# First attention: four strips as one row read by 64 rows, transposes by halves of the array, contexts and side work spread over steps

## The chip, the cores and the metric

The kernel runs on one core of a Trainium2 chip. The time is device microseconds of one execution; several executions give a median. A profiled execution of the same kernel gives the trace that is read here. PE is TensorE (PEld its weight loads), DVE VectorE, ACT ScalarE, POOL GpSimd, SP the engine whose queue issues most DMAs. All data is fp32.

## The reference

Two transformer layers over x of shape (8, 512, 256): attention, feed-forward, attention, mixture of experts, each added to x behind a layer norm. The change is in the first attention alone, which has 16 heads of 16 and a relative position term:

```python
q, k, v = split_heads(x @ Wq + bq), split_heads(x @ Wk + bk), split_heads(x @ Wv + bv)
scores = einsum('bhqd,bhkd->bhqk', q, k) / scale
c2p = take_along_axis(einsum('bhqd,hpd->bhqp', q, pos_k), c2p_pos, -1)   # pos by q - k
p2c = take_along_axis(einsum('bhkd,hpd->bhkp', k, pos_k), p2c_pos, -1)
scores = scores + (c2p + swapaxes(p2c)) / scale
ctx = einsum('bhqk,bhkd->bhqd', softmax(scores), v)
out = layernorm(ctx @ Wo + bo + x) * ln_scale + ln_bias
```

The position depends on q - k only, in logarithmic buckets, and is constant beyond 128 tokens on either side.

## The kernel before

**Steps.** The first attention, `_l0_attention`, is 256 steps, written out in a fixed order (`manual_schedule`): batch b (8), group g of four heads (4), block i of 128 tokens (4), pair p of heads (2). `strips(u)` runs five steps ahead (AHEAD = 5) of `products(n)`.

**Strips (L302 to L363).** For two heads and one block, PE multiplies q and k of 128 tokens with the position table: four strips of 256 columns in two PSUM banks (L314, `pa`). ACT copies them to `strip` (L321). Column 255 of a strip is a constant for keys far away on one side; POOL multiplies it with a triangle (L324, `own`). SP writes the strips to one of four DRAM buffers `shift` (L331): each strip is an area of its own, with rows of 2 W = 512 elements, of which 255 are written. One step later `read` (L340) reads them back with a row step of one element less, so that row r comes back moved by r: `winp` for keys and `winc` for queries, 128 rows, two heads, 256 or 384 columns. The columns outside of a strip are zeros, written once at the start (L143). One step after that, POOL adds `own` to both (L351).

**Products (L365 to L385).** PE multiplies q and k into two score banks `sc` (L371, in two parts; the strips' matmuls stand between them) and adds the moved key strips by transposing matmuls of `winp` (L383, `near_keys`). Heads lie 32 rows apart, so these matmuls use 32 rows of the array each.

**Weights.** DVE adds `winc` and takes the row's extreme in one operation (L397, `e` and `low`), ACT takes the exponential (L400). A step later PE transposes `e` in four 128x128 blocks for each head (L407, `turned`), DVE copies the bank (L409, `et`), and every second step PE multiplies four heads' weights with v (L418, `weigh`, 16 matmuls to 32 columns of the array each).

**Side work.** Behind each step the program runs one waiting piece: first from `urgent` (the next group's projections, L290, two halves), else from `side` (values L273, the divide L450, outputs L463, layer norms, turns L267). `later(k, ...)` puts pieces there that may run k steps later. A layer norm's `measure` and `norm` take four blocks of 128 tokens in one piece. At the start of groups 0 and 3 all that waits is run at once.

DMAs are issued by SP in program order. PSUM: two banks each for `pa`, `sc`, `et_ps`, one for the contexts and one for side work.

Of the kernel before, what the change touches and what calls it, by code (L numbers as in the profile page):

```python
# [12 lines left out]
F32 = mybir.dt.float32  # L13
# [15 lines left out]
W = 256  # L29
WIN = 3 * P  # L30
# [31 lines left out]
def _normalize(nc, out, x, mv, rstd, i):  # L62
    nc.vector.tensor_scalar(out, x, mv[:, i, 0:1], rstd[:, i : i + 1], ALU.subtract, ALU.mult)  # L63

# [26 lines left out]
def _l0_attention(nc, tc, a, x, ident, mhalf, carry, prefetch):  # L91
# [6 lines left out]
    with ExitStack() as ctx:  # L98
# [16 lines left out]
        bias = wp.tile([P, 4, NG], F32, tag="bias", name="bias")  # L115
        xns = [carry.tile([P, NT, H], F32, tag=f"xn{n}", name=f"xn{n}") for n in range(2)]
        xnT = carry.tile([P, NK, S], F32, tag="xnT0", name="xnT")
        shift = [dram.tile([4 * P, 2 * W], F32, tag=f"shift{n}", name=f"shift{n}") for n in range(NSHIFT)]
        with tc.tile_pool(name="a_pos", bufs=1) as pp:
# [3 lines left out]
            tail = pp.tile([P, 2], F32, tag="tail", name="tail")  # L123
# [6 lines left out]
            nc.scalar.dma_start(tail, a["tail"])  # L130
# [9 lines left out]
            zeros = pp.tile([P, 2 * W], F32, tag="zeros", name="zeros")  # L140
            nc.gpsimd.memset(zeros, 0.0)
            for d in shift:
                nc.sync.dma_start(  # L143
                    d.rearrange("(q p) w -> p q w", p=P), zeros.unsqueeze(1).to_broadcast([P, 4, 2 * W])
                )
# [6 lines left out]
            def normalized(pool, b):  # L152

                stats = []

                def measure():
                    stats.extend(_batch_norm_stats(nc, pool, [x[b][:, t, :] for t in range(NT)], 1e-5, mhalf))

                def norm():
                    for t in range(NT):  # L160
                        _normalize(nc, xns[b % 2][:, t, :], x[b][:, t, :], *stats, t)

                return measure, norm

            for f in normalized(pp, 0):
                f()
# [19 lines left out]
            for g in range(NG):  # L186
                for t, dst in ((0, posc), (1, posp)):
# [8 lines left out]
                    nc.vector.tensor_copy(dst[:, g, W - 1 : W], tail[:, t : t + 1])  # L196
# [37 lines left out]
        winc = []  # L234
        for n in range(2 * NT):
            w = wp.tile([P, 2, S], F32, tag=f"winc{n}", name=f"winc{n}")
            nc.gpsimd.memset(w, 0.0)
            winc.append(w)
# [10 lines left out]
        sm, wins, totals = {}, {}, {}  # L249
# [33 lines left out]
        def project(b, g):  # L283
# [16 lines left out]
            return [partial(half, wq, 0, -SCALE), partial(half, wk, 2, 1.0)]  # L300
# [5 lines left out]
        def strips(u, between=None):  # L306
# [12 lines left out]
            st = sb.tile([P, 4, W], F32, tag="strip", name="strip")  # L319
            for j in range(2):  # L320
                nc.scalar.copy(st[:, 2 * j : 2 * j + 2, :].rearrange("p t w -> p (t w)"), pas[j])  # L321
# [5 lines left out]
                st[:, :, W - 1 : W].rearrange("p (j t) o -> p t j o", t=2).to_broadcast([P, 2, 2, P]),  # L327
# [3 lines left out]
            nc.sync.dma_start(  # L331
                bass.AP(d.tensor, d.offset + P + 1, [[2 * W, P], [2 * W * P, 4], [1, W - 1]]), st[:, :, : W - 1]
            )
            wc = winc[u % (2 * NT)]
            wk_ = sb.tile([P, 2, WIN], F32, tag="winp", name="winp", bufs=8)

            def read():
                lo, hi, c0, c1 = near(i)
                for t, dst in ((1, wk_[:, :, c0:c1]), (0, wc[:, :, lo * P : hi * P])):
                    nc.sync.dma_start(  # L340
                        dst,
                        bass.AP(
                            d.tensor,
                            d.offset + t * 2 * W * P + P + c0,
                            [[2 * W - 1, P], [4 * W * P, 2], [1, c1 - c0]],
                        ),
                    )
# [55 lines left out]
        def turned(e):  # L403
            et_ps = ps_t.tile([P, S], F32, tag="pst", name="et_ps")
            for m in range(NT):
# [1269 lines left out]
```

## Time and profile before

| | |
|---|---|
| three runs | 2128.27, 2134.96, 2135.02 us; median 2134.96 |
| profiled execution | 2132.52 us, of it the span of the trace 2130.7 us |
| first attention | to about 1,124 us of the span |
| mean granted TensorE clock | 0.961 over the span |
| busy time, PE / DVE / ACT / POOL | 92% / 65% / 52% / 53% of the span |
| DMA by SP's queue | 373904 packets, 401.93 MB, 62.4% of 16 engines over the span |
| HBM | 238.99 MB read, 202.19 MB written |

The page gives busy shares over the whole span and over 40 equal slices (a digit is tenths). The groups give, for a line, an engine and a shape, the busy time, the mean ns of one, and the idle time before it with what ended it. Matmuls overlap, so one instruction's duration is longer than its share of the stream; what a part costs PE is read from the starts in the timeline.

### The profile page before, as it was taken

How to read it: one execution, taken by the hardware profiler on the slowest of the kernel's cores; microseconds unless marked ns; L12 is line 12 of the kernel's file. 1: busy time of each engine (PE TensorE's matmuls, PEld its weight loads, DVE VectorE, ACT ScalarE, POOL GpSimd, SP SyncE). 2: the span in 40 equal slices, each digit the busy share in tenths (PEclk: the TensorE clock that was granted, in tenths of full speed). 3: DMA queues.
4: the chain of work that ended last, by engine and by line, in shares of the span. 5: the costliest groups of instructions: out<-in, count | busy, mean ns of one | idle time of the engine just before them, and what ended most of it. 6: DMA issues, size and time to landing. Idle time of an engine off the chain costs nothing.

```text
span 2130.7 us, 46004 instructions
## 1 busy us (share of the span) xinstructions
PE 1963.5 (92%) x15908; PEld 1415.5 (66%) x15908; DVE 1393.8 (65%) x3715; ACT 1104.7 (52%) x2366; POOL 1138.3 (53%) x1328
## 2 busy tenths in 40 slices
PE   7999999999999999999998999989988777499997
PEld 4777677777776777777775666645555445388886
DVE  3576776767767677686777555347876776356666
ACT  2776767667676766767662122244444333144443
POOL 5666766767667676676753111013544443355555
PEclk7999999999999999999999999999999987699999
DMA  8998989898898989989883544900111114556788
GB/s 273 316 293 275 283 278 299 271 290 282 269 299 276 277 280 282 295 270 293 275 283 93 165 142 126 87 0 29 46 40 43 49 42 167 198 166 209 253 259 268
DMA packets 388916, 444.21 MB, mean 208 GB/s; under 512 B 43344, under 2 KB 367952, under 8 KB 388688
## 3 DMA queue, kind: packets, MB, share of 16 engines
q1 hardware_dynamic: 373904, 401.93, 62.4%
q0 software_dynamic: 13824, 38.29, 4.9%
q8 instruction: 130, 2.13, 0.4%
q10 hardware_dynamic: 960, 1.05, 0.1%
q14 instruction: 98, 0.80, 0.1%
HBM read 238.99 MB, written 202.19 MB: 207 GB/s over the span
## 4 chain that ended last, share of the span: by engine, by line
PE 32%; DVE 10%; issue 4%; ACT 2%; SPq 1%; DMA 1%; POOL 1%; POOLq 0%; DVEq 0%; ACTq 0%
PE pge L1430 7%; PE po L674 5%; PE poe L1448 3%; PE ph L666 3%; PE pq L925 2%; PE ao L1015 2%; PE ptr L1422 2%; DVE prod L786 1%; PE pv L937 1%; DVE value L786 1%; PE po L1044 1%; SPq L1387 1%; PE ps L962 1%; DVE st L53 1%; DVE xn L63 1%
## 5 line engine op out<-in xcount | busy, mean ns | idle before, releaser
L397 DVE CUSTOM_DVE_ANT_0 e<-sc,winc 128x512 f32<-128x512 f32 x512 | 333.2, 688 | 293.9 <-PE sc L383 127.5
L400 ACT ACTIVATE e<-e,low 128x512 f32<-128x512 f32 x512 | 365.7, 716 | 110.1 <-DVE low L397 105.6
L324 POOL TENSOR_TENSOR own<-aside,strip 128x512 f32<-128x512 f32 x256 | 268.9, 1051 | 205.1 <-ACT strip L321 178.9
L321 ACT COPY strip<-pa 128x512 f32<-128x512 f32 x512 | 275.7, 592 | 185.7 <-issue 54.6
L371 PE MATMUL sc<-sm,sm 32*128 32x256 f32 (+3 forms) x1792 | 326.0, 439 | 19.2 <-DVE low L397 19.2
L409 DVE COPY et<-et_ps 128x512 f32<-128x512 f32 x512 | 328.7, 683 | 0.3 <-PE et_ps L407 0.2
L314 PE MATMUL pa<-pos,sm 32*128 32x256 f32 x2048 | 299.1, 407 | 1.7 <-ACT sm L298 1.0
L407 PE MATMUL et_ps<-ident,e 128*128 128x128 f32 x2048 | 268.2, 274 | 0.2 <-DVE et L409 0.2
L869 POOL DMA_INDIRECT rows<-pay,slot x128 | 141.9, 1109 | 233.0 <-issue 218.2
L371 PEld LDWEIGHTS sc<-sm,sm 32*128 32x128 f32 x1792 | 162.2, 184 | 130.3 <-DVE low L397 51.8
L407 PEld LDWEIGHTS et_ps<-ident,e 128*128 128x128 f32 x2048 | 234.3, 142 | 0.6 <-ACT e L400 0.4
L351 POOL TENSOR_TENSOR winp<-winp,own 128x256 f32<-128x256 f32 x256 | 186.9, 730 | 76.8 <-DMA winp<-shift 63.0
L869 POOL DMA_INDIRECT results<-y,r x160 | 156.8, 980 | 122.8 <-ACT y L1450 74.7
L351 POOL TENSOR_TENSOR winc<-winc,own 128x256 f32<-128x256 f32 x256 | 187.2, 731 | 40.0 <-DMA winc<-shift 37.4
L383 PE MATMUL sc<-ident,winp 128*128 128x128 f32 x1280 | 199.6, 285 | 5.8 <-DMA winp<-shift 5.8
L383 PEld LDWEIGHTS sc<-ident,winp 128*128 128x128 f32 x1280 | 136.4, 141 | 80.7 <-issue 59.6
L314 PEld LDWEIGHTS pa<-pos,sm 32*128 32x128 f32 x2048 | 179.8, 187 | 12.5 <-ACT strip L321 2.4
L58 POOL TENSOR_TENSOR rstd<-var,mhalf 128x4 f32<-128x4 f32 x40 | 44.8, 1121 | 249.3 <-DVE var L56 226.2
L1430 PE MATMUL pge<-store,rT 128*128 x640 | 168.2, 386 | 2.5 <-DVE rT L1424 0.9
L418 PE MATMUL ctx_ps<-et,v 128*32 128x128 f32 x4096 | 140.0, 277 | 0.2 <-DVE et L409 0.2
L669 ACT ACTIVATE hT<-ph,b 128x512 f32<-128x512 f32 x64 | 44.0, 687 | 166.0 <-PE ph L666 166.0
L290 PE MATMUL pq<-xnT,wqk 128*128 128x512 f32 x256 | 126.0, 614 | 3.1 <-DVE xnT L78 3.1
(216 smaller groups left out, 3337.3 us busy)
## 6 DMA issues: line engine op xcount, KB each, us to landing
shift<-strip SPq DMA_DIRECT2D x256, 510.0 KB
winp<-shift SPq DMA_DIRECT2D x128, 384.0 KB
winc<-shift SPq DMA_DIRECT2D x128, 384.0 KB
winp<-shift SPq DMA_DIRECT2D x128, 256.0 KB
winc<-shift SPq DMA_DIRECT2D x128, 256.0 KB
rows<-empty SPq DMA_DIRECT2D x8, 2640.0 KB
r<-rows SPq DMA_DIRECT2D x160, 132.0 KB
z<-results SPq DMA_DIRECT2D x32, 512.0 KB
```

What stands on the lines that cost most here:

```text
L314: nc.tensor.matmul(pa[:, t * W : (t + 1) * W], src[rs, i * P : (i + 1) * P], pos[rs, g, :], start=True, stop=True)
L321: nc.scalar.copy(st[:, 2 * j : 2 * j + 2, :].rearrange("p t w -> p (t w)"), pas[j])
L324: nc.gpsimd.tensor_tensor(own, aside.unsqueeze(2).to_broadcast([P, 2, 2, P]), st[:, :, W - 1 : W].rearrange("p (j t) o -> p t j o", t=2).t ...
L351: nc.gpsimd.tensor_tensor(dst, dst, own[:, t], ALU.add)
L371: nc.tensor.matmul(sc[:, c0:c1], s[side_][rs, cut : cut + P], s[2 + side_][rs, c0:c1], start=c0 == 0, stop=False, skip_group_check=True,)
L383: nc.tensor.matmul(sc[:, m * P : (m + 1) * P], wins[n + 2 * (m - i)][1][:, j, (i - m + 1) * P : (i - m + 2) * P], ident, start=False, stop ...
L397: nc.vector.tensor_tensor_reduce(e, sc, wins[n][0][:, j, :], 1.0, -LOW, ALU.add, ALU.min, low)
L400: nc.scalar.activation(e, e, AF.Exp, bias=low, scale=-1.0, accum_out=totals[b, g // 2][:, i, r : r + 1])
L407: nc.tensor.transpose(et_ps[:, ms], e[:, ms], ident)
L409: nc.vector.tensor_copy(et, et_ps)
L869: ins = nc.gpsimd.indirect_dma_start(to, bass.IndirectOffsetOnAxis(ap=index, axis=0), source, None, bounds_check=last)
L1430: nc.tensor.matmul(pg[:, :H], rT[:, k * P : (k + 1) * P], w[:, k * H : (k + 1) * H], start=k == 0, stop=k == NK - 1)
```

## The change

- Strips: `st` is one of three fixed tiles with a pitch of PITCH = 320 for each strip, the last 64 columns zero. A token's four strips are one DRAM row of 1,280 elements, written as a whole. The zeros between strips take the place of the zeroed areas; one row of zeros is written at the start.
- `read` makes two DMAs of 64 rows for each of `winp` and `winc`, 192 to 320 columns each, instead of one of 128 rows.
- `winp` are eight fixed tiles, `winc` are slices of four wider tiles; all are cleared once.
- The far-away constants come from a new piece `left`: eight matmuls for each batch and group, with q or k as weights and `tail` (four columns) as moving data, and one DVE copy. `own` reads it instead of the strip.
- `turned` takes both heads of a step: rows 0 to 63 of each block are transposed into one bank, rows 64 to 127 into the other.
- `weigh` runs half of its matmuls in each of two steps.
- `measure` and `norm` take two blocks each, as separate pieces; the delays of side work are changed; `left` is the third urgent piece of a group.

```diff
-        shift = [dram.tile([4 * P, 2 * W], F32, tag=f"shift{n}", name=f"shift{n}") for n in range(NSHIFT)]
+        shift = [dram.tile([P + 1, 4 * PITCH], F32, tag=f"shift{n}", name=f"shift{n}") for n in range(NSHIFT)]
...
-            zeros = pp.tile([P, 2 * W], F32, tag="zeros", name="zeros")
+            zeros = pp.tile([1, 4 * PITCH], F32, tag="zeros", name="zeros")
             nc.gpsimd.memset(zeros, 0.0)
             for d in shift:
-                nc.sync.dma_start(
-                    d.rearrange("(q p) w -> p q w", p=P), zeros.unsqueeze(1).to_broadcast([P, 4, 2 * W])
-                )
+                nc.sync.dma_start(d[:1, :], zeros)
...
-                    nc.vector.tensor_copy(dst[:, g, W - 1 : W], tail[:, t : t + 1])
...
+        for n in range(3):
+            w = wp.tile([P, 4, PITCH], F32, tag=f"strips{n}", name="strip")
+            nc.gpsimd.memset(w, 0.0)
+            strip_rows.append(w)
...
+            def left():
+
+                pl = misc("pl")
+                for i in range(NT):
+                    for t in range(2):
+                        c = (2 * i + t) * 4
+                        nc.tensor.matmul(
+                            pl[:, c : c + 4], out[2 * t][:, i * P : (i + 1) * P], tail[:, t, :], start=True, stop=True
+                        )
+                lefts[b, g] = w = sb.tile([P, NT, 2, 4], F32, tag="left", name="left")
+                nc.vector.tensor_copy(w.rearrange("p i t r -> p (i t r)"), pl[:, : 8 * NT])
+
-            return [partial(half, wq, 0, -SCALE), partial(half, wk, 2, 1.0)]
+            return [partial(half, wq, 0, -SCALE), partial(half, wk, 2, 1.0), left]
...
-            st = sb.tile([P, 4, W], F32, tag="strip", name="strip")
+            st = strip_rows[u % 3]
             for j in range(2):
-                nc.scalar.copy(st[:, 2 * j : 2 * j + 2, :].rearrange("p t w -> p (t w)"), pas[j])
+                nc.scalar.copy(st[:, 2 * j : 2 * j + 2, :W], pas[j].rearrange("p (t w) -> p t w", t=2))
...
-                st[:, :, W - 1 : W].rearrange("p (j t) o -> p t j o", t=2).to_broadcast([P, 2, 2, P]),
+                lefts[b, g][:, i, :, 2 * p : 2 * p + 2].unsqueeze(3).to_broadcast([P, 2, 2, P]),
...
-            nc.sync.dma_start(
-                bass.AP(d.tensor, d.offset + P + 1, [[2 * W, P], [2 * W * P, 4], [1, W - 1]]), st[:, :, : W - 1]
-            )
+            nc.sync.dma_start(d[1:, :], st.rearrange("p n w -> p (n w)"))
...
             def read():
-                lo, hi, c0, c1 = near(i)
-                for t, dst in ((1, wk_[:, :, c0:c1]), (0, wc[:, :, lo * P : hi * P])):
-                    nc.sync.dma_start(
-                        dst,
-                        bass.AP(
-                            d.tensor,
-                            d.offset + t * 2 * W * P + P + c0,
-                            [[2 * W - 1, P], [4 * W * P, 2], [1, c1 - c0]],
-                        ),
-                    )
+                lo, hi, first, end = near(i)
+                for t, dst, o in ((1, wk_, 0), (0, wc, (i - 1) * P)):
+                    for p0 in range(0, P, 64):
+                        c0, c1 = max(first, p0), min(end, p0 + 2 * P + 64)
+                        nc.sync.dma_start(
+                            dst[p0 : p0 + 64, :, o + c0 : o + c1],
+                            bass.AP(
+                                d.tensor,
+                                d.offset + 4 * PITCH + t * PITCH + c0 - 1 + p0 * (4 * PITCH - 1),
+                                [[4 * PITCH - 1, 64], [2 * PITCH, 2], [1, c1 - c0]],
+                            ),
+                        )
...
-        def turned(e):
-            et_ps = ps_t.tile([P, S], F32, tag="pst", name="et_ps")
-            for m in range(NT):
-                ms = slice(m * P, (m + 1) * P)
-                nc.tensor.transpose(et_ps[:, ms], e[:, ms], ident)
-            et = sb.tile([P, S], F32, tag="et", name="et", bufs=6)
-            nc.vector.tensor_copy(et, et_ps)
-            return et
+        def turned(es):
+            banks = [ps_t.tile([P, S], F32, tag="pst", name="et_ps") for _ in range(2)]
+            for j, e in enumerate(es):
+                for m in range(NT):
+                    for f, bank in enumerate(banks):
+                        rs, c = slice(64 * f, 64 * f + 64), (j * NT + m) * 64
+                        nc.tensor.transpose(bank[:, c : c + 64], e[rs, m * P : (m + 1) * P], ident[rs, rs])
+            et = sb.tile([P, 2, 2, NT, 64], F32, tag="et", name="et", bufs=4)
+            for f, bank in enumerate(banks):
+                nc.vector.tensor_copy(et[:, f].rearrange("p j m q -> p (j m q)"), bank)
+            return [et[:, :, j] for j in range(2)]
...
-                    later(3, *[partial(out, t, misc, sb) for t in range(NT)])
-                    later(9, partial(measure, misc, sb))
-                    later(12, partial(norm, misc, sb))
+                    later(3, *[partial(f, misc, sb) for f in fs])
...
+                        if g == NG - 3 and b + 1 < B:
+                            ready = normalized(sb, b + 1)
+                            later(4, *ready[:2])
                         if g == NG - 2 and b + 1 < B:
-                            measure, norm = normalized(sb, b + 1)
-                            later(1, measure)
-                            later(3, norm, *[partial(turn, b + 1, k) for k in range(NK)])
+                            later(2, *ready[2:], *[partial(turn, b + 1, k) for k in range(NK)])
...
                 if n % 2 and len(ets) >= 4:
-                    weigh(n - 3, [ets.popleft() for _ in range(4)])
+                    four = [ets.popleft() for _ in range(4)]
+                    weigh(n - 3, four, 0)
+                elif n % 2 == 0 and n >= 4:
+                    weigh(n - 4, four, 1)
```

Here `fs` is the list of the batch's four outputs, then `measure` and `norm` for blocks 0 and 1 and for blocks 2 and 3; `weigh(n, ets, part)` runs the matmuls of key blocks 2 part and 2 part + 1.

## The prediction

> **What bounds the kernel now.** I read the page first, then the busy time by stretches, the groups by shape within 150 to 1100 us, the PE timeline of single steps, and the waits in the same window.
>
> ```profile
> PE 1963.5 (92%) x15908; PEld 1415.5 (66%) x15908; DVE 1393.8 (65%) x3715; ACT 1104.7 (52%) x2366; POOL 1138.3 (53%) x1328
> ...
> PE   7999999999999999999998999989988777499997
> ...
> DMA  8998989898898989989883544900111114556788
> ```
>
> ```profile
> 500.00:600.00 100.00, 96.48 (x1102) 71.68 (x1096) 72.11 (x181) 69.15 (x156) 70.15 (x88) 1.00 0.90 281
> ```
>
> The first attention is the first 21 slices, some 1,120 us with its start. In it two resources are nearly full: PE (96%, at full granted clock) and the DMA engines (0.90). DVE, ACT and POOL stand near 70%. The stage is 256 steps; steps start every 4.19 us on average (236 steps between 110 and 1100 us). The step is read from the PE timeline:
>
> ```profile
> 605.06 0.87 PE L383 MATMUL sc<-ident,winp 128*128 128x128 f32 x6
> 605.77 1.04 PE L407 MATMUL et_ps<-ident,e 128*128 128x128 f32 x8
> 606.64 0.60 PE L450 MATMUL spread<-ident,wide 128*128 128x128 f32 x4
> 607.17 0.52 PE L371 MATMUL sc<-sm,sm 32*128 32x256 f32 x2
> ...
> 608.28 1.01 PE L383 MATMUL sc<-ident,winp 128*128 128x128 f32 x6
> 609.13 1.04 PE L407 MATMUL et_ps<-ident,e 128*128 128x128 f32 x8
> 610.10 1.08 PE L418 MATMUL ctx_ps<-et,v 128*32 128x128 f32 x32
> 611.11 1.13 PE L463 MATMUL po<-wo,cn 128*128 128x256 f32 x4
> 612.17 0.59 PE L371 MATMUL sc<-sm,sm 32*128 32x384 f32 x2
> ```
>
> Start to start this gives the price of each part: products and strips 1.08 to 1.11 us; near keys 0.71 (four matmuls at an end block: 0.49); eight transposes 0.87 when whole-array work follows and 0.97 when another tiling follows; contexts 1.01, every second step; an output 1.06. So each change of tiling costs about 0.1 us. A projection half is 1.81 to 1.91 by the same reading. A step without side work should be 2.65 or 3.66 us of PE, 3.1 on average, yet pairs of such steps average 3.47 each: DVE holds the two score banks. After near keys start, e of head 0 begins 0.8 us later, two passes of 688+83 ns follow, and only then may the next products start (about 2.2 us for the second head), plus 1.05 us of products: a loop of 3.2 us.
>
> ```profile
> L397 DVE CUSTOM_DVE_ANT_0 e<-sc,winc 128x512 f32<-128x512 f32 x452 | 294.2, 688 | 262.1 <-PE sc L383 115.2 <-ACT strip L321 98.8 <-DMA winp<-shift 28.4
> L409 DVE COPY et<-et_ps 128x512 f32<-128x512 f32 x454 | 291.5, 683 | 0.0
> ...
> L407 PEld LDWEIGHTS et_ps<-ident,e 128*128 128x128 f32 x1808 | 207.2, 142 | 0.0
> ...
> L371 PEld LDWEIGHTS sc<-sm,sm 32*128 32x128 f32 x1584 | 141.4, 184 | 117.0 <-DVE low L397 45.5 <-issue 43.8 <-DVE et L409 25.9
> ...
> L418 PEld LDWEIGHTS ctx_ps<-et,v 128*32 128x32 f32 x3624 | 92.9, 110 | 19.4 <-issue 19.2
> ```
>
> ```profile
> POOL own L324 <- ACT strip L321: 155.2, 136, 3.0
> ...
> PEld sc L371 <- DVE low L397: 45.5, 113, 1.4
> ...
> ACT strip L321 <- POOL winc L351: 41.7, 31, 1.9
> ```
>
> PE's stalls in the stage (what each part takes over its undisturbed time) come to about 95 us in 990, most of them behind DVE low. PE waits for DMA hardly at all. So it is a PE stage with a DVE loop close under it.
>
> **The change part by part** (durations from the profiled execution, 2132.5 us; it stands 2.4 us under the median).
>
> *Transposes by halves.* Eight transposes of 128 columns become sixteen of 64 rows into 64 columns, in pairs on the two halves of the array. The row first: weight loads take 184 ns (128 columns) and 110 ns (32 columns) for ordinary fp32 matmuls, so 0.77 ns a column over a fixed 85 ns; a transpose's load takes 142, so only 57 ns for its 128 columns. The products show loads and matmuls on different row groups starting 7 ns apart, four at once. A pair then costs the larger of a 57 ns load and 64 columns, half of the 107 ns that 128 take: 55 ns. Eight pairs are 0.44, with an exposed first load and a change of tiling behind it 0.60. [...] By the row the gain is 0.33 us a step[...] Whole-array near keys now stand before a half-array tiling, which adds about 0.1 us there.
>
> *Contexts over two steps.* 0.43 of streaming plus 0.15 per half: 1.17 for the two, against 1.01; +0.08 a step. Side work always follows them and pays its first load (+0.05 on average).
>
> So PE without side work is 1.08+0.69+0.60+0.58 = 2.95. With a projection half (1.91) 4.86, before 5.01; with values or an output (1.06) 4.02, before 4.22 and 4.12. A projection gains 0.15, the others 0.1 to 0.2.
>
> *left.* For each batch and group eight new fp32 matmuls, 128x128 weights against four columns, run as sixteen. The nearest row is the router's matmul, 128x128 weights against 32 columns:
>
> ```profile
> 1437.65 1.99 PE pl L1086 x16
> ```
>
> [...] It falls in the third step of each group, where there was no PE side work: 2.95+1.92 = 4.87 against 3.47, +1.40, for 31 of them 43 us. The first runs before the loop at half clock: 3.4 us more. Nothing hides it, as PE is the bound. If it fell in true idle time only the excess would count, some 30 us; with the router's own 1.99 it is 46. The copy on DVE is 32 columns wide and costs at most 0.2 us.
>
> *Side work even.* The instruction order of the changed program gives, for 32 steps: 8 projection halves, 4 left, 4 values, 4 outputs, 4 measures and 4 norms of two tiles each, one divide alone, and at the last group's start two turns and a divide drained at once behind a norm; three steps are bare. DVE has 2.91 us in any step; a measure of two tiles adds 1.33 (four took 2.4), a norm 1.46 (2 x 733 ns). Steps of that kind in a row are DVE-bound at 4.2 to 4.4 whether the lump is two tiles or four. Sum for 32 steps: 8x4.87 + 4x4.87 + 8x4.05 + bare and divide 13.4 + measure, measure, norm 11.2 + norm, measure, measure, norm, norm with the drain 22.6 = 138.0. The same 32 steps before, 586.9 to 722.3 us, took 135.4; the stage's mean is 134.1. I take +3 per batch, +24 over eight.
>
> *Own without the strip.* POOL's biggest wait (155 us) goes, and ACT's strip copy no longer waits for POOL. What is late next is DVE low again; POOL was no PE stall, so I count nothing. If it did hold PE, up to 10 us are gained.
>
> *DMA.* Per step, writes go from 512 packets of 1,020 B to 128 of 5,120; reads stay at 512 packets, of 768 to 1,280 B instead of 1,024 or 1,536. Together 1,212 KB instead of 1,178 and 640 packets instead of 1,024. The page's q1 row gives 57 ns for a packet of 1,075 B. By bytes the share rises from 0.90 to 0.93, by packets it falls to about 0.6; I take 0.85 to 0.9, and as PE does not wait there, no time. SP issues five DMAs a step instead of three: at 0.36 to 0.45 us each it is busy some 2.1 of 4.2 us, since it already waits 436 us for the strip. Two reads more stand in front of the next write on SP, about 0.9 us; their users (winp add, winc add, near keys) have most of a step's slack. If that slack is gone, 0.2 us a step, 50 us.
>
> *Start.* The 4 MB of zeros go, but the first strip write at 40.06 us waits for ACT, not DMA. POOL clears some 8 us more; it was through at 30 and the first own came at 40, so this is hidden; 0 to 4 us.
>
> Sum: +24+3 = +27 on 2132.5, or 2160 against the median.
>
> **The rivals.**
> 1. The stalls go (faster). If the even steps and the freed ACT keep DVE out of the way, a batch falls to the PE sums alone: 32x2.95 + 8x1.91 + 4x1.92 + 8x1.06 + 2 = 128.2, minus 48 us over the stage at best: 2087; half of that, 2110, is likelier. For it: 95 us of stalls are there. Against: DVE's own work is the same. It decides when a step with a measure or norm stays under about 3.9 us.
> 2. Halves do not overlap (slower). If two half transposes take 107 ns each, 0.44 us more in some 20 of 32 steps and less in the rest: +90, 2245. Against: four row groups do overlap now.
> 3. The longer chain of DMAs on SP comes late: +40 to +60, 2205.
> The transposes doing what they say and left being free would give about 2120; it lies with rival 1.
>
> **How the numbers follow.** The forecast 0.47, stalls gone 0.28, halves serial 0.13, DMA late 0.12. Some 0.3% (6 us) is what a measurement here can tell from no change. The forecast's own spread (2135 to 2190) puts a tenth within it and a little below. Faster 0.29, same 0.09, slower 0.62. The range 2098 to 2230 leaves out the far ends of rivals 1 and 2.
>
> **What would show it.** Right: sixteen transposes in about 0.6 us, contexts 0.58 a step, a new PE group of 512 short matmuls with about 1.9 us for sixteen, DVE low still the first wait of the products, POOL's wait for the strip gone. Wrong: transposes at 0.9 us or more (rival 2); near keys waiting for DMA winp (rival 3); PE stalls under 0.2 us a step and a stage shorter than 1,060 us (rival 1).

## The result, and the profile after

| | before | after |
|---|---|---|
| median of four runs on one chip | 2133.04 us | 2211.86 us |
| lowest and highest | 2128.27 to 2135.02 | 2210.97 to 2214.98 |
| profiled span | 2130.7 us | 2210.6 us |
| granted TensorE clock over the span | 0.961 | 0.943 |

The changed kernel is slower: ratio 1.0376, 95% interval 1.0353 to 1.0398, or 79 us, where 27 were forecast. The page after shows a stage as full as before. First the totals, then rows of the 40 slices and the queue:

```profile
PE 2019.9 (91%) x18468; PEld 1407.5 (64%) x18468; DVE 1393.9 (63%) x3755; ACT 1108.2 (50%) x2366; POOL 1154.4 (52%) x1351
...
PEclk7899999999999999999998999999999988699999
DMA  5988978878889798897986454830111112656888
...
q1 hardware_dynamic: 281688, 406.71, 60.1%
```

PE has 56 us more of busy time (1963.5 before). The DMA row has lost some nines, as forecast. The clock row looks harmless: its digits are tenths of slices of 55 us. One line for 860 us of the stage says more (columns: busy us of PE, PEld, DVE, ACT, POOL, then granted clock, DMA share, GB/s). Before, then after:

```profile
200.00:1060.00 860.00, 836.07 (x9544) 625.37 (x9543) 611.06 (x1506) 595.45 (x1347) 599.42 (x748) 1.00 0.91 283
```

```profile
200.00:1060.00 860.00, 823.89 (x10838) 576.23 (x10840) 573.32 (x1446) 562.42 (x1266) 565.32 (x708) 0.97 0.86 273
```

In the same 860 us DVE ran 1446 instructions instead of 1506: fewer steps. PE's idle time in them has grown only from 24 to 36 us, but its granted clock is 0.97 instead of 1.00. That is the first thing that the prediction did not reckon with. The parts of a step that it did price are in the PE timeline, in a step with `left` and one with `values` behind it:

```profile
606.81 0.88 PE L411 MATMUL sc<-ident,winp 128*128 128x128 f32 x6
607.62 0.72 PE L439 MATMUL et_ps<-ident,e 64*128 64x64 f32 x16
608.27 0.65 PE L451 MATMUL ctx_ps<-et,v 128*32 128x128 f32 x16
608.84 1.95 PE L321 MATMUL pl<-tail,sm 128*128 128x4 f32 x16
610.72 0.38 PE L399 MATMUL sc<-sm,sm 32*128 32x128 f32 x2
...
612.06 1.54 PE L411 MATMUL sc<-ident,winp 128*128 128x128 f32 x6
613.53 1.12 PE L439 MATMUL et_ps<-ident,e 64*128 64x64 f32 x16
614.58 0.77 PE L451 MATMUL ctx_ps<-et,v 128*32 128x128 f32 x16
615.27 1.13 PE L288 MATMUL pv<-wv,xnT 128*128 128x256 f32 x4
```

Start to start: near keys 0.81 us, sixteen half transposes 0.65, half the contexts 0.57, `left` 1.88. All four are what the prediction said, to 0.05 us (near keys with its 0.1 for the change of tiling). In the next step near keys take 1.47 and the transposes 1.05: a stretch at half clock, from 611.5 to 614.9 us. The clock records hold 17 such stretches, 75 us, between 80 and 1150 us of the span; before held 4, 17 us.

The waits within 150 to 1100 us (total us, times, longest), two of before and then those of after:

```profile
POOL winp L351 <- DMA winp<-shift: 50.1, 66, 2.8
...
PE sc L383 <- DMA winp<-shift: 5.2, 8, 2.1
```

```profile
POOL winp L379 <- DMA winp<-shift: 154.8, 127, 6.5
...
PEld sc L399 <- DVE et L442: 55.5, 103, 0.8
PEld sc L399 <- DVE low L425: 24.1, 52, 1.3
...
PE sc L411 <- DMA winp<-shift: 5.5, 10, 1.3
...
POOL own L351 <- DVE left L325: 2.3, 4, 0.9
```

POOL's wait for the strip (155 us before) is gone, but its wait for the reads of `winp` has grown from 50 to 155 us; PE waits for them 5.5 us, 5.2 before. DVE's `et` copy, not `low`, is now the first wait of the products, and the two are small.

Means over six batches (32 steps each) give the balance. Rows are the groups of the prediction's sum; the last column is a kernel from below in which all but one of these batches' half-clock stretches are gone (e14).

| steps of a batch, us | before | forecast | after | e14 |
|---|---|---|---|---|
| 8 projection halves | 40.1 | 39.0 | 41.5 | 40.7 |
| 4 `left` (the same places before) | 12.7 | 19.5 | 19.9 | 20.1 |
| 4 outputs, 4 values (same places) | 31.3 | 32.4 | 33.9 | 32.6 |
| bare and divide (3, 4, 5, 31) | 16.4 | 13.4 | 13.1 | 13.1 |
| 13 to 15, measure, measure, norm | 12.6 | 11.2 | 10.4 | 10.3 |
| 19 to 23, with the drained pieces | 21.3 | 22.6 | 24.7 | 23.7 |
| sum | 134.4 | 138.0 | 143.5 | 140.6 |

### The profile page after: what moved, and what is told of

Its sections match the earlier page's. It is cut to its first block, busy times and chain, and to the rows that moved or that the text cites. A ratio compares the mean times of both kernels' runs of the same rounds, so it can differ in the third digit from the quotient of the medians.

```text
span 2210.6 us, 51476 instructions
## 1 busy us (share of the span) xinstructions
PE 2019.9 (91%) x18468; PEld 1407.5 (64%) x18468; DVE 1393.9 (63%) x3755; ACT 1108.2 (50%) x2366; POOL 1154.4 (52%) x1351
## 3 DMA queue, kind: packets, MB, share of 16 engines
q10 hardware_dynamic: 1088, 1.05, 0.2%
## 5 line engine op out<-in xcount | busy, mean ns | idle before, releaser
L399 PE MATMUL sc<-sm,sm 32*128 32x256 f32 (+3 forms) x1792 | 330.5, 453 | 10.8 <-DVE low L425 10.3
L341 PE MATMUL pa<-pos,sm 32*128 32x256 f32 x2048 | 310.0, 422 | 0.7 <-ACT strip L348 0.7
L351 POOL TENSOR_TENSOR own<-aside,left 128x512 f32<-128x512 f32 x256 | 267.1, 1044 | 18.1 <-DVE left L325 5.4
L411 PE MATMUL sc<-ident,winp 128*128 128x128 f32 x1280 | 209.4, 295 | 14.2 <-DMA winp<-shift 13.8
L411 PEld LDWEIGHTS sc<-ident,winp 128*128 128x128 f32 x1280 | 143.1, 146 | 95.3 <-issue 66.3
L341 PEld LDWEIGHTS pa<-pos,sm 32*128 32x128 f32 x2048 | 184.9, 194 | 11.1 <-issue 2.0
L439 PE MATMUL et_ps<-ident,e 64*128 64x64 f32 x4096 | 185.7, 231 | 1.1 <-DVE et L442 1.1
L439 PEld LDWEIGHTS et_ps<-ident,e 64*128 64x128 f32 x4096 | 150.3, 141 | 46.8 <-ACT strip L348 23.7
L59 POOL TENSOR_TENSOR rstd<-var,mhalf 128x2 f32<-128x2 f32 (+1 forms) x56 | 51.0, 912 | 239.5 <-DVE var L57 217.5
L451 PE MATMUL ctx_ps<-et,v 128*32 128x128 f32 x4096 | 166.5, 281 | 0.5 <-DVE et L442 0.5
L305 PE MATMUL pq<-xnT,wqk 128*128 128x512 f32 x256 | 131.7, 637 | 2.4 <-DVE wqk L208 2.4
```

Of the source, the lines that this page charges most:

```text
L341: nc.tensor.matmul(pa[:, t * W : (t + 1) * W], src[rs, i * P : (i + 1) * P], pos[rs, g, :], start=True, stop=True)
L351: nc.gpsimd.tensor_tensor(own, aside.unsqueeze(2).to_broadcast([P, 2, 2, P]), lefts[b, g][:, i, :, 2 * p : 2 * p + 2].unsqueeze(3).to_broa ...
L399: nc.tensor.matmul(sc[:, c0:c1], s[side_][rs, cut : cut + P], s[2 + side_][rs, c0:c1], start=c0 == 0, stop=False, skip_group_check=True,)
L411: nc.tensor.matmul(sc[:, m * P : (m + 1) * P], wins[n + 2 * (m - i)][1][:, j, (i - m + 1) * P : (i - m + 2) * P], ident, start=False, stop ...
L439: nc.tensor.transpose(bank[:, c : c + 64], e[rs, m * P : (m + 1) * P], ident[rs, rs])
```

## The experiments

Every kernel ran beside the kernel before on the same chip, whose median there was 2126 to 2136 us; ratios are to it, with the 95% interval. On that scale after is 1.0376, about 2206 us where before takes 2126. "Half clock" is the time at half granted clock between 80 and 1150 us of the span (before 17 us, after 75).

| kernel | ratio | half clock, us |
|---|---|---|
| e1 after, left only once | 1.0089 (1.0069 to 1.0108) | 28 |
| e2 after, side schedule of before | 1.0350 (1.0327 to 1.0373) | 89 |
| e3 before, halves alone | 0.9969 (0.9960 to 0.9979) | 48 |
| e4 before, halves and split contexts | 0.9948 (0.9931 to 0.9965) | 38 |
| e5 after, strips of before | 1.0397 (1.0380 to 1.0415) | 109 |
| e6 before, left alone | 1.0233 (1.0215 to 1.0252) | 27 |
| e7 after, whole-array transposes | 1.0548 (1.0526 to 1.0570) | 82 |
| e8 after, PE kept busy in the drained step | 1.0323 (1.0304 to 1.0341) | 48 |
| e9 e4 with output norm by pairs | 0.9915 (0.9900 to 0.9929) | 38 |
| e10 before, left and split contexts | 1.0478 (1.0459 to 1.0497) | 75 |
| e11 after, contexts unsplit | 1.0217 (1.0198 to 1.0235) | 72 |
| e12 after, another filling for left | 1.0321 (1.0303 to 1.0338) | 42 |
| e13 after, left with 64 columns | 1.0328 (1.0306 to 1.0349) | 48 |
| e14 e8 and e13 together | 1.0249 (1.0227 to 1.0271) | 14 |
| e15 e9, PE kept busy before a turn | 0.9912 (0.9892 to 0.9932) | 24 |

**e1: left only once.**

```diff
-            return [partial(half, wq, 0, -SCALE), partial(half, wk, 2, 1.0), left]
+            return [partial(half, wq, 0, -SCALE), partial(half, wk, 2, 1.0)] + ([left] if (b, g) == (0, 0) else [])
...
-                lefts[b, g][:, i, :, 2 * p : 2 * p + 2]...
+                lefts[0, 0][:, i, :, 2 * p : 2 * p + 2]...
```

> The kernel after, but left's matmuls run only once, for the first group, and every own is built from that first left (so the own-block term of the other groups is not the reference's). It takes 31 pieces of 1.92 us of PE work away, and with four places a batch free only the divide is still drained at the last group's start. Theory A (left costs its PE time, and the rest of the loss is the drained norm-turn-turn-divide step with the half-clock stretches behind it): left 43 to 46 us plus 25 to 30 us for drain and clock, so about 2140 us, and no more half-clock stretches in the stage than the four of before. Rival C (the thinner PE work of the halves itself lowers the granted clock): about 2165 us, with the half-clock stretches still there. Rival B (the reads by 64 rows come late): 2165 to 2170.

Ratio 1.0089, 2146 us: 61 us less than after, near theory A's 2140. A batch takes 134.6 us; steps in `left`'s places fall from 19.9 to 14.5, the group with the drained pieces from 24.7 to 22.2, and steady batches have 0 to 3.4 us of half clock. So `left` with what follows from it is three quarters of the loss; part of that is that its four places a batch come free and only the divide is still drained. Without it the change still loses about 19 us, mostly before step 32, which starts at 198.3 us instead of 184.2.

**e2: the side schedule of before**, `measure` and `norm` over four blocks, with before's delays:

```diff
-                    later(3, *[partial(f, misc, sb) for f in fs])
+                    later(3, *[partial(out, t, misc, sb) for t in range(NT)])
+                    later(9, partial(measure, misc, sb))
+                    later(12, partial(norm, misc, sb))
...
-                            later(2, *ready[2:], *[partial(turn, b + 1, k) for k in range(NK)])
+                            later(1, measure)
+                            later(3, norm, *[partial(turn, b + 1, k) for k in range(NK)])
```

> The kernel after with the side schedule of the kernel before: statistics and normalisation over four tiles in one step, with the delays of before; left, halves, contexts and strip rows stay. Nothing is drained at the last group's start any more. Theory A: 2180 us (2172 to 2190), half-clock stretches of the stage down from 85 us to about 20, and no step of 10 us. Rival C or B: the stretches stay, 2200 to 2212.

Nothing is drained any more, yet the time is 1.0350, not distinguishable from after, and half clock rises to 89 us. This refutes theory A in its first form: the drained step is not what brings the half-clock stretches, or not alone. Nor does idle PE grow with them: between 200 and 1060 us PE idles 26 us at a clock of 0.96, in after 36 us at 0.97.

**e3: halves alone.** Only `turned` (L431 to L443), the context operand and the call are taken over:

```diff
+                        nc.tensor.transpose(bank[:, c : c + 64], e[rs, m * P : (m + 1) * P], ident[rs, rs])
...
-                        et[:, m * P : (m + 1) * P],
+                        et[:, :, m, :],
```

> The kernel before with one thing of the change alone: the transposes by halves of the array (contexts unsplit, no left, the old strips, the old side schedule). Sixteen short transposes should take 0.64 us instead of eight in 0.87 to 0.97, 0.3 us of PE a step. If PE bounds the step throughout, 256 x 0.3 = 75 us, 2058; if the DVE loop of the scores holds the steps without side work, only the 20 of 32 steps with PE work gain: about 2085 to 2110. Rival C (halves lower the clock): 2130 or more with several times the half-clock time of before.

The mechanism works as in after; the group's PE row, x3664 within 150 to 1100 us:

```profile
L411 PE MATMUL et_ps<-ident,e 64*128 64x64 f32 x3664 | 167.1, 232 | 0.0
```

But the gain is 6.6 us, not 20 to 40. In the kernel before bare steps end with the DVE loop (3.59 us before, 3.37 with halves, at full clock), and half-clock time grows from 17 to 48 us. PE time freed in front of DVE turns into idle time: 32 us between 200 and 1060 us where before has 24, at a clock of 0.98 instead of 1.00.

**e5: the old strips.** Strip tile, write, reads and the zeroed DRAM as before; `own` still from `left`:

```diff
-            st = strip_rows[u % 3]
+            st = sb.tile([P, 4, W], F32, tag="strip", name="strip")
...
-            nc.sync.dma_start(d[1:, :], st.rearrange("p n w -> p (n w)"))
+            nc.sync.dma_start(
+                bass.AP(d.tensor, d.offset + P + 1, [[2 * W, P], [2 * W * P, 4], [1, W - 1]]), st[:, :, : W - 1]
+            )
...
-                    for p0 in range(0, P, 64):
```

> The kernel after with the strips stored and read as before: written in 512 pieces of 1,020 B, read by two DMAs of 128 rows, three DMAs a step on SP instead of five, DRAM cleared at the start; own still from left. Theory A: no gain, 2205 to 2220 us (the clearing may cost a few us at the start). Rival B: 20 us or more come back, 2190 or less, and POOL's waits for DMA winp and winc fall from 238 us to the 60 of before or less.

1.0397: no gain; the interval overlaps that of after. But the sum hides two things that work against each other. Half clock is 34 us longer than in after, and at full clock e5 is the faster one: over the thirty steps of a batch that both run at full clock its means add up to 1.2 us less, 10 us over eight batches. Of this 0.8 us lies at places 8 and 9 of a batch (steps counted from 0), two projection halves, where near keys wait for the reads in after and not in e5. One such step, at place 8, in after and then in e5:

```profile
809.34 0.33 PE L411 MATMUL sc<-ident,winp 128*128 128x128 f32 x1
810.97 0.52 PE L411 MATMUL sc<-ident,winp 128*128 128x128 f32 x3 [1.30 <-DMA winp<-shift]
```

```profile
815.98 0.66 PE L406 MATMUL sc<-ident,winp 128*128 128x128 f32 x4
```

So rival 3 of the prediction, reads that come late, is there, but at 10 us at most and not 40 to 60. SP was also busier than forecast; the timeline of its queue in after (start, duration, x2 for two issues):

```profile
484.31 0.54 SPq L358 DMA_DIRECT2D shift<-strip  x1
485.02 1.47 SPq L368 DMA_DIRECT2D winp<-shift  x2
486.60 1.22 SPq L368 DMA_DIRECT2D winc<-shift  x2
```

That is 3.2 us of a 4.5 us step where 2.1 had been estimated. Whether the issues on SP or the 64-row transfers make the reads late was not tried apart.

**e4, e6, e7, e8**: the two other parts alone, halves undone, and PE kept busy.

e4 is e3 with the contexts in two steps:

```diff
-                    weigh(n - 3, [ets.popleft() for _ in range(4)])
+                    four = [ets.popleft() for _ in range(4)]
+                    weigh(n - 3, four, 0)
+                elif n % 2 == 0 and n >= 4:
+                    weigh(n - 4, four, 1)
```

> The kernel before with the halves and the contexts spread over two steps, no left, old strips, old side schedule. The halves alone gave 0.9969. Theory A (the loop of scores, e and low on DVE takes what the halves free, and even steps sit closer to it): bare steps fall from 3.37 to about 3.1 us (8 a batch, 2 us), the split's own cost of 0.08 us a step takes 2.5 us back, so 2112 to 2125 us, ratio 0.993 to 1.000. Rival: the gain of even steps is full, 2105 or less.

0.9948, or 2115: some 5 us better than halves alone (the intervals overlap at their ends). Bare steps fall to 3.15 us, as theory A had it.

e6 adds `left` and `own` from it to the kernel before, as in the change:

```diff
-            return [partial(half, wq, 0, -SCALE), partial(half, wk, 2, 1.0)]
+            return [partial(half, wq, 0, -SCALE), partial(half, wk, 2, 1.0), left]
...
-                st[:, :, W - 1 : W].rearrange("p (j t) o -> p t j o", t=2).to_broadcast([P, 2, 2, P]),
+                lefts[b, g][:, i, :, 2 * p : 2 * p + 2].unsqueeze(3).to_broadcast([P, 2, 2, P]),
```

> The kernel before with left alone (own built from it; whole-array transposes, old strips, old side schedule). Left by its PE time: its step from 3.2 to 4.95 us, four a batch, plus 3.7 us at the start: 2126 + 50 = 2176. If left also brings the half-clock stretches (one window of 3.41 us at half clock after projection, projection, left): three a batch, some 3 us a batch more, 2190 to 2200. If the halves bring them, the half-clock time of the stage stays near before's 17 us and the time at 2176.

2176, as forecast from its PE time, and 27 us of half clock. `left` by itself costs little more than it was priced at (50 us against 46).

e7 puts eight whole-array transposes back into after:

```diff
-                        nc.tensor.transpose(bank[:, c : c + 64], e[rs, m * P : (m + 1) * P], ident[rs, rs])
+                nc.tensor.transpose(et_ps[:, ms], e[:, ms], ident)
```

> The kernel after with whole-array transposes again, eight of 128x128 a step; all else as after. If the halves are worth their PE time where PE bounds the step (0.3 us for the transposes less 0.1 for the near keys in front of them, all 32 steps): 2206 + 45 = 2250. If they are mostly hidden, as in the kernel before with halves alone (-7 us): 2213. If halves cause the half-clock stretches, those fall from 75 us to 20 and the time goes below 2206.

2244, 37 us more than after, near the full worth (2250). So the halves are worth 7 us in the kernel before and 37 us here: with `left` and split contexts nearly every step is bound by PE. They do not bring the half-clock stretches (82 us without them).

e8 gives PE something to do while the drained pieces wait:

```diff
+                            warm = ps_a.tile([P, S], F32, tag="psa", name="warm") if side else None
+                            count = 5
                             while side:
+                                for _ in range(count):
+                                    nc.tensor.matmul(warm[:, :W], ident, posc[:, 0, :], start=True, stop=True)
+                                count = 2
                                 side.popleft()[1]()
```

> The kernel after with idle-time matmuls (ident by 256 columns into an unused bank, five ahead of the first drained piece and two ahead of each other one) so that PE is not idle while it waits for the drained norm, turns and divide. Theory: [...] the stretches in the drained step and in the projection after it go (5 us of half clock a batch), the drained step falls from 10.2 to 8.5 to 9.5 us and the time from 2206 to about 2190. Rival (the stretches come from something else): stretches and step stay, 2204 to 2212.

The drained step and the projection behind it, by windows, in after:

```profile
584.47:594.75 10.28, 6.74 (x65) 4.49 (x65) 6.97 (x15) 4.68 (x11) 8.26 (x11) 0.82 0.96 283
594.75:600.95 6.20, 6.20 (x54) 3.54 (x53) 3.20 (x7) 2.60 (x6) 2.49 (x3) 0.75 0.35 118
600.95:610.72 9.77, 9.77 (x123) 6.91 (x122) 5.02 (x12) 7.50 (x16) 3.95 (x5) 1.00 0.87 263
610.72:616.34 5.62, 5.62 (x60) 3.96 (x59) 2.79 (x7) 2.59 (x6) 3.02 (x4) 0.70 0.71 226
```

and the first two in e8:

```profile
579.79:589.57 9.78, 9.38 (x82) 7.05 (x83) 7.38 (x15) 4.68 (x11) 8.23 (x11) 1.00 0.90 293
589.57:594.36 4.79, 4.79 (x53) 2.74 (x52) 3.20 (x7) 2.60 (x6) 2.45 (x3) 1.00 0.39 138
```

In after PE idles 3.5 us of the drained step, waiting for DVE's norm and for the copies of the two turns; clock 0.82, and 0.75 in the projection step behind. With idle-time matmuls both steps have full clock, the projection takes 4.79 instead of 6.20 us and the kernel 11 us less. So one kind of stretch does follow idle PE. The fourth line of after is another kind: clock 0.70, no idle before it.

**e9, e10, e11.** e9 is e4 with the output's `measure` and `norm` in pairs of blocks; e10 is e6 with split contexts (as in e4; to make room it also has fewer buffers for some small tiles of the layer norms and the divide, which was not tried alone); e11 is after with that diff undone. e9's edit:

```diff
-                    later(3, *[partial(out, t, misc, sb) for t in range(NT)])
-                    later(9, partial(measure, misc, sb))
-                    later(12, partial(norm, misc, sb))
+                    later(3, *[partial(f, misc, sb) for f in fs])
```

> The kernel before with halves, split contexts (0.9948 so far) and the two-tile measures and norms of the output alone (x's stay at four tiles; no left, old strips). Without left nothing of it is drained. In the kernel after with left run once the three steps of output norm took 10.8 us against 12.5 here, so 1.7 us a batch: ratio 0.988 to 0.991, 2101 to 2107. Rival (the smaller lumps only move DVE's work to the next step): 0.994 to 0.996.

0.9915, 2110: a gain of 7 us, just short of the 0.988 to 0.991 that was expected; the three steps fall from 12.5 to 10.7 us, but the group of x's norm rises by 1.5.

> The kernel before with left and the contexts over two steps (whole-array transposes, old strips, old side schedule). Without the split it took 2176. The split's worth with halves was 5 us: 2171. If left together with evenly filled steps is what brings the half-clock windows that no idle precedes, two or more a batch show here after projection, projection, left: 2175 to 2190. If the halves or the strip rows are needed for them: none, 2165 to 2176.

1.0478, 2229: far outside. The split that gained 5 us with halves and without `left` costs 52 us here.

> The kernel after with the contexts of both pairs in one step, every second step; all else as after (2206 beside this kernel before). Price of the split: 0.08 us of PE a step, 20 us in all, against steadier steps. If the even filling is worth more than its PE time, 2212 to 2225 here; if not, 2190 to 2200. If the half-clock windows without idle before them need the split, they vanish (34 us of half clock less).

1.0217, 2175: undoing the split gives 34 us back (1.6% of 2126), better than either expectation; half clock stays (72 us in the profiled execution, the slowest of four: 2185 beside 2170 to 2175). Step times at full clock account for part of both runs. With whole-array transposes a pair `left` step plus next bare step takes 5.21+3.33 split and 4.44+3.76 unsplit, two `values` steps 8.78 and 8.45: 0.33 us a pair, 42 us over the 128 pairs of the stage, of e10's 52 (its half clock grew too, from 27 to 75 us). With halves it is 4.98+3.10 against 4.40+3.53, 8.32 against 8.18: 0.14 a pair, 2.2 us a batch. Even steps help pairs of bare steps (3.37 us each in e3, 3.15 in e4), where the DVE loop ends one of the two. `left` fills just those: it runs two steps into a group of eight, on an even step, and unsplit contexts fall on odd ones. So 18 of e11's 34 us are the split's own PE time; the rest I can't assign, as its outputs and drained pieces also fall one place earlier.

**e12: another filling.** What is it in `left`'s place that halves the clock?

```diff
+            def fill():
+                pl = misc("pl")
+                for k in range(NK):
+                    nc.tensor.matmul(pl, wq[:, k, 4 * g : 4 * g + 4, :]..., xnT[:, k, :], start=k == 0, stop=k == NK - 1)
...
+            return [partial(half, wq, 0, -SCALE), partial(half, wk, 2, 1.0), left if (b, g) == (0, 0) else fill]
```

> The kernel after with left's matmuls only for the first group (every own built from that first left, so the own-block term of the other groups is not the reference's), and in left's place, for the other groups, two matmuls of a projection's form (128x128 weights, 512 columns) whose result nobody reads: 1.9 us of PE as before, of another form. It asks whether the half-clock windows without idle before them come from left's own form (sixteen loads against four columns) or from any PE work in that place. Any PE work: 2200 to 2212, windows in the steps behind left's place as in after (10 us of half clock a batch). Left's form: those windows go, about 2190.

1.0321, or 2194 where before takes 2126 as above (beside this kernel before took 2136): between the two, nearer to the second. The same steps as in e8's windows settle it: here the `values` step behind the filling takes 4.16 us at a clock of 1.00, where after has 5.62 at 0.70 behind `left`. The drained step, in which PE idles 3.9 us, keeps a clock of 0.83, and the projection behind it 0.74. Of the 12 us, 3 are the start, as first strips run at 39.8 instead of 42.65 us.

**e13, e14, e15**: a `left` of more columns; the same with e8's edit; PE kept busy in the fastest version. e13's edit:

```diff
-                        c = (2 * i + t) * 4
+                        c = (2 * i + t) * 64
...
-                            pl[:, c : c + 4], out[2 * t][:, i * P : (i + 1) * P], tail[:, t, :], start=True, stop=True
+                            pl[:, c : c + 64], out[2 * t]..., tail[:, t, :].unsqueeze(2).to_broadcast([P, 4, 16]), ...
```

> The kernel after with each of left's moving columns repeated sixteen times (64 columns against the same sixteen loads), so that left streams more in the same time; its copy reads every sixteenth column. Ratio of after: 1.0376. [...] the half-clock windows without idle before them go, left's step stays at 4.98 to 5.15 us, ratio 1.031 to 1.034. If the loads or the place bring them: they stay, 1.037 to 1.042.

1.0328, in the first of the two ranges; of the 10 us up to 3 may be the start, as first strips run at 39.8 us here. Same loads, same place, 5.03 instead of 4.98 us for the step, sixteen times the columns: half clock falls from 75 to 48 us. The steps of the timeline above, with full clock in the `values` step, 4.15 us at 1.00 where after has 5.62 at 0.70:

```profile
592.52:602.35 9.83, 9.83 (x124) 6.93 (x123) 5.02 (x12) 7.49 (x16) 3.95 (x5) 1.00 0.85 264
602.35:606.50 4.15, 4.15 (x59) 2.99 (x58) 2.49 (x7) 2.60 (x6) 1.69 (x2) 1.00 0.67 219
```

> The wide left and the idle-time matmuls in the drained step together. Each alone is worth about 0.5% of the time, if they add up 1.026 to 1.029, and half-clock time under 3 us a batch; that measures the clock's share of the 79 us as about 20 to 25 us. If the summation of steps at full clock is right (4.2 us a batch), up to 33 us: 1.022.

1.0249, 1.3% under after, 27 us: the two remedies add up and give a little more than their sum (21 us). Clock in the stage:

```profile
200.00:1060.00 860.00, 844.40 (x11159) 595.12 (x11156) 581.85 (x1470) 574.46 (x1294) 577.09 (x723) 1.00 0.87 279
```

So about 27 of the 79 us are clock, and 53 remain at full clock. The half-clock time agrees: after has 58 us more of it than before, and at a granted clock of 0.50 that is a loss of 29 us at most, an estimate from the clock records.

e15's edit, on e9:

```diff
+            if now >= 0 and k == 0:
+                for _ in range(4):
+                    nc.tensor.matmul(pt[:, :W], ident, posc[:, 0, :], start=True, stop=True)
```

> The fastest version (halves, split contexts, output norm by pairs; 0.9915) with four idle-time matmuls ahead of each batch's first turn, where PE waits 1.6 us for the norm on DVE and a half-clock window follows. If the window goes: 1 us a batch, 0.987 to 0.989. If DVE bounds those steps: 0.991 to 0.993.

0.9912 against 0.9915: no difference. Half clock falls to 24 us, but the steps are DVE's (the first turn's step takes 6.06 us at full clock, 5.96 in e9). The fastest version is e9, or e15, about 18 us under the kernel before.

## Why the prediction was wrong

The direction was right, and so were the prices of most parts; the size was off by 52 us. The step that failed most is one that was not written down: the sum carried the full granted clock of the kernel before over to the kernel after, and half clock took about 27 us of the 52 (e14). Behind it come terms of the sum that were too small: the projection halves with the late reads, and the drained pieces. By its own steps:

- *Transposes by halves*: right, by the row of the trace. Sixteen take 0.64 to 0.65 us, and the pairs overlap: in the step above the two of a pair start 4 to 13 ns apart and the pairs, behind the first, 60 to 62 ns apart, where whole transposes of before start 109 ns apart. Rival 2 (2245) is out. The prediction's 107 ns for 128 columns is a quarter of the 429 ns from one 512-column matmul of before to the next. Only the worth depends on the cover: 7 us in the kernel before (e3), 37 in after (e7).
- *Contexts over two steps*: 0.57 a step, right. "+0.08 a step" is 0.07 with halves at full clock (e11 against after). As a part alone it costs up to 34 us in after and gains 5 without `left` (e4).
- *left*: 1.88 us against 1.92, the author's estimate beside the router's 1.99, and its step 4.98 against 4.87, its copy 0.19 us on DVE against 0.2; alone it costs 50 us (e6) against 46. Right. That e1 takes away 61 has two causes beyond this price: the clock (at most 10 us, e13) and the pieces that are no longer drained (24.7 to 22.2 us a batch).
- *Projection 4.87*: mis-sized in two of eight. At full clock most take 4.79 to 5.02. The half at place 8 takes 4.9 to 6.3 in after and 4.79 to 4.80 in e5, where its near keys do not wait for the reads; the half at place 16 takes 5.40 or more, as its products wait for DVE, which runs a measure (1.4 us) just ahead. All eight together are +1.7 us a batch (e14's column).
- *The drained pieces, 22.6*: mis-sized. 24.7 us, 23.7 with full clock. The norm, two turns and a divide wait for one another: PE first for DVE's norm, then twice for the copy out of the one bank, 3.5 us.
- *Measures and norms by two blocks*: a little better than priced, 10.4 against 11.2 (a norm's operation takes 0.49 to 0.62 us in after where 0.73 was taken from before); bare steps 13.1 against 13.4.
- *The granted clock*, 1.00 in the stage before, was carried over without a word; it is 0.97 in after. This cost about 27 us (e14).
- *Start*: 3 us were forecast, it took 6.1 up to the first strip. PE's timeline of after has the 3.7 us of `left`, as priced, at a granted clock of 0.50, and ahead of it a wait of the first projection for the setup's weights:

```profile
27.40 1.66 PE L305 MATMUL pq<-xnT,wqk 128*128 128x512 f32 x2 [2.36 <-DVE wqk L208]
...
38.99 3.73 PE L321 MATMUL pl<-tail,sm 128*128 128x4 f32 x16 [1.61 <-ACT sm L313]
42.65 2.08 PE L341 MATMUL pa<-pos,sm 32*128 32x256 f32 x8
```

  POOL clears strips between the products that make `wqk`; that this is the wait's cause was not tried. Other kernels with this start had their first strips at 39.8 to 43.8 us, so it varies.
- *DMA*: the share was right (0.86 against 0.85 to 0.9), "no time" was not. The new strips cost 1.2 us a batch at full clock, 10 us in all (e5 against after), and SP's issues take 3.2 us a step instead of 2.1.
- *Rival 1's sum* comes to 127.8, not 128.2, which changes nothing.
- *From 138.0 to +3*: the sum stood 3.6 above the six batches' mean before; 5 us over eight batches went by rounding.

The balance: clock 27, eight batches times 2.6 us at full clock 21 (some 10 of them the new strips), rounding 5, start 3: 56 for the 52 missed. Of the signs named for being right only DVE `low` as first wait failed; of those for being wrong, near keys do wait for the reads. Rival 1's stalls did go (bare steps 3.08 instead of 3.6 us). Rival 3's 2205 is near the time by luck: its cause is worth 10 us of the 79 at most.

## What to carry to other kernels

A piece of work priced by its time alone was not fully priced here: `left`'s sixteen matmuls of four columns took 1.88 us, close to their price, but in after the `values` step behind them took 5.62 us at a clock of 0.70, and 4.15 at 1.00 behind a `left` of 64 columns (e13). Look at the granted clock in windows of a few us before and after, never only in the row of tenths. And evening out steps was worth something here only while some steps waited for another engine (the split gains 5 us in e4 and costs 52 in e10); count how many of those are left once the change's own additions have filled them.

## What the runs showed of the hardware that was not expected

In the traces of before and after the granted clock is either full or one half. Between 80 and 1150 us the half-clock stretches of both last 3.41 or 6.83 us: four in before (17 us), 17 in after (75 us). The clock and PE records show what ran in the 3.41 us ahead of each. In before PE had idled 1.2, 1.2, 1.9 and 3.4 us of them. In after there are two kinds: ahead of seven stretches PE had idled 1.7 to 2.2 us; ahead of the other ten it had not idled at all, and in each of them `left` ran for 1.8 to 1.95 us. So at most 2.2 us of the 3.41 ahead of a stretch of after were idle, and ahead of ten none. Not every `left` has a stretch behind it: of the 30 between 80 and 1150 us of after, these ten have.

The runs take the two kinds apart. With PE kept busy in the drained step (e8), this step and the projection behind it have a clock of 1.00 instead of 0.82 and 0.75. With two projection matmuls (e12) or 64 columns (e13) in place of the four-column `left`, the `values` step has 1.00 instead of 0.70. With both edits (e14) 860 us of the stage have 1.00 instead of 0.97, and half clock is 14 us. The same four-column `left` in the kernel before brings little of it (e6: 27 us, a clock of 0.99 over the 860 us), and more once contexts are split (e10: 75 us, 0.96). What makes this difference was not shown.
